# Two-layer graph attention on one core: a small addition after each of layer 0's gathers, and an order made from 16-byte ranges

## The chip, the cores and the metric

The kernel runs on one NeuronCore of a Trainium2 chip. A core has five engines that run their own instruction queues side by side: TensorE (PE, with its weight loads shown as PEld), VectorE (DVE), ScalarE (ACT), GpSimd (POOL) and SyncE (SP, which here only issues transfers). They signal each other through semaphores. Data lies in SBUF (128 partitions), products go to PSUM, and DMA engines move data between SBUF and HBM. The metric is the device time of one execution in microseconds, as the median of several runs.

## The reference, cut to what matters

Two layers on 2708 nodes of width 256, with one dense 2708 x 2708 adjacency matrix in which few entries are not zero:

```python
x = layernorm(x + gnn0(x, adj))    # layer 0
x = layernorm(x + gnn1(x, adj))    # layer 1

def gnn0(h, adj):                  # node_adj and edge_adj are both adj
    d = diag(adj); a = adj with its diagonal set to zero
    edge_output = gru_cell(a @ h, h, edge weights)
    support = mean over 3 heads of  (softmax(mask(e_head), axis=1) * a) @ (h @ W_head)
    node_output = gru_cell(support, h, node weights)
    return d * edge_output + d * node_output
    # a > 0 takes e_plus; entries of a are never negative

def gnn1(x, adj):                  # 4 heads of 64 columns
    h = x @ W;  e = leaky_relu(s_src[i] + s_dst[j]), masked where adj <= 0.5
    return softmax(e, axis=0) summed over i with h, per head
```

The adjacency is sparse and its nonzeros thin out with the node's number, so the kernel finds the rows that a block of columns needs and fetches only those.

## The kernel before, in words

The fast path (a general path stands behind it for other data) has four stages.

*Loading and listing.* The transposed adjacency is read once in three parts of up to 1024 columns (63 large loads on SP's queue). ScalarE and VectorE turn each piece into signs and bits, TensorE makes the softmax logits and denominators. For 51 blocks of columns of layer 0 (`BLOCKS0`) and 32 of layer 1 (`BLOCKS1`), `listed` (line 716) makes lists of the row numbers that are not all zero: counts by a scan and small products, then large comparisons on VectorE (tiles f_lists), products onto `lst` and `rk`, and an index table (`idx`). There are eight such batches for layer 0 and five for layer 1.

*Layer 0's sums.* The blocks are worked off in groups of 512 columns, in the order 4, 3, 2, 1, 0, 5. For each list of 128 rows two gathers are issued on GpSimd, an indirect DMA each: the raw adjacency values of those rows in the block's columns (`fetch_raw`, line 841, into f_raw, or f_ah for the first 16) and the rows of x with their head weights (`fetch_rows`, line 1063, from the table f_T0 into f_xg). There are 131 of each kind. The raw ring holds 40 pieces, the row ring (`xg_ring`, line 625) four buffers of two row sets. `layer0` (line 1074) multiplies on VectorE (tile f_four) and TensorE adds up in PSUM (tiles acc). Blocks with many full rows take the first of them without a gather.

*Cells and norm.* When a group's sums are complete, `cells_and_norm` (line 1130) makes the products with the head weights and the two gated cells (PE tiles side), the gates on ScalarE and VectorE, the layer norm, and layer 1's table f_T1. For each block of 128 nodes GpSimd adds the result to a running sum (f_xacc) and adds a bias (f_low).

*Layer 1.* 96 gathers (`fetch_h`, line 1344) fetch rows of f_T1 into buffers that take the place of the lists, VectorE makes the masked weights (again shown as f_lists), TensorE adds up, and the result is normed and written.

*What sets the order.* The program is not emitted in the order of its text. Every call is kept in an `Order` (its `add` is reached from line 375, which is why the profile shows that line nearly everywhere). `issue` (line 223) finds which call depends on which from the ranges of SBUF that they touch, gives each a duration (`duration`, line 180), and lists all calls by a forward and backward pass repeated twelve times; the best list is emitted, and each engine gets its calls in that order. `spans` (line 134) turns an access into ranges, counted in cells of 32 bytes: two calls that touch the same cell are taken to depend on each other. The synchronisation in the emitted program is made afterwards from the accesses themselves. Calls recorded inside `R.together()` stay next to each other. A gather is taken to cost 1.36 us:

```python
        if engine == "gpsimd":
            if method == "indirect_dma_start":
                return 1.36
            return (n * (4.0 if method == "tensor_add" else 0.8) + 60) / 960.0
```

All gathers go through one helper, `gathered` (line 812), called from the three fetch functions.

Of the kernel before, what the change touches and what calls it, by code (L numbers as in the profile page):

```python
# [14 lines left out]
U32 = mybir.dt.uint32  # L15
# [7 lines left out]
P = 128  # L23
# [49 lines left out]
def _size(ap):  # L73
    n = 1
    for d in ap.shape[1:]:
        n *= d
    return n


def _width(dt):  # L80
    return {F32: 4, I32: 4, U32: 4, BF16: 2, F16: 2, U16: 2, F8: 1}[dt]
# [6 lines left out]
class Order:  # L88
# [44 lines left out]
    @staticmethod  # L133
    def spans(ap):

        name, pat, wide = ap.tensor.name, [tuple(d) for d in ap.ap], _width(ap.dtype)
        if name.startswith("in_"):
            return name, []
        space = str(ap.space)
        if "PSUM" in space:  # L140
            return name, [(0, 1)]
        if "DRAM" in space:
            at, cell = ap.offset, 1024
        else:
            step = pat[0][0]
            at, cell = (ap.offset % step if step else ap.offset), 32
            pat = pat[1:]
        run, outer = 1, []
        for s, n in sorted((abs(s), n) for s, n in pat if s and n > 1):
            if s <= run + cell // wide:  # L150
                run = s * (n - 1) + run
            else:
                outer.append((s, n))
        starts = [at]
        for s, n in outer:
            starts = [a + k * s for a in starts for k in range(n)]
        out = []
        for a in sorted(starts):
            lo, hi = a * wide // cell, (a + run) * wide - 1
            hi = hi // cell + 1  # L160
            if out and lo <= out[-1][1]:
                out[-1] = (out[-1][0], max(hi, out[-1][1]))
            else:
                out.append((lo, hi))
        return name, out
# [14 lines left out]
    def duration(self, call):  # L180
        engine, method, args, kw = call
        outs, ins = self.touched(call)
        out = outs[0]
        n = max([_size(out)] + [_size(a) for a in ins if method in ("tensor_reduce", "bn_stats")])
        if engine == "tensor":
            moving = kw["rhs"] if method == "matmul" else args[1]
            still = kw["lhsT"] if method == "matmul" else args[1]
            cols = _size(moving) if method == "matmul" else P
            if _width(moving.dtype) == 4:
                if method == "transpose":  # L190
                    return 0.2
                return max(4 * cols + 2 * _size(still), 800 if _size(still) > 96 else 500) / 2400.0
            return max(cols, 108) / 2400.0 + 0.01
        if engine == "vector":
            wide = [a for a in outs + ins if _size(a) > 1]
            fast = all(_width(a.dtype) == 2 for a in wide) or (
                method == "tensor_scalar" and all("PSUM" not in str(a.space) for a in wide)
            )
            if method in ("tensor_tensor_scan",):
                n *= 1.5  # L200
            if method == "reciprocal":
                n *= 8
            if method in ("bn_stats", "tensor_reduce", "memset", "copy_predicated"):
                fast = False
            return ((n / 2 if fast else n) + 150 + (60 if method == "scalar_tensor_tensor" else 0)) / 960.0
        if engine == "scalar":
            extra = sum(isinstance(kw.get(k), bass.AP) for k in ("scale", "bias"))
            return (n + 224 + 93 * extra) / 1200.0
        if engine == "gpsimd":
            if method == "indirect_dma_start":  # L210
                return 1.36
            return (n * (4.0 if method == "tensor_add" else 0.8) + 60) / 960.0
        return 0.45

# [185 lines left out]
def fast_path(ctx: ExitStack, tc: tile.TileContext, i: dict, out: bass.AP, bad: bass.AP):  # L400
    nc = tc.nc
    R = Order(nc)
    V, S, G, T, Q = R.vector, R.scalar, R.gpsimd, R.tensor, R.sync
    x, xT_in, adj, adjT = i["x"], i["xT"], i["adj"], i["adjT"]
# [26 lines left out]
    def home(name, shape, dt=F32):  # L431
        return const.tile(shape, dt, name=name)
# [31 lines left out]
    T0 = dram.tile([N, TW0], F32, name="f_T0")  # L464
    T1 = dram.tile([N, TW1], U32, name="f_T1")
# [52 lines left out]
    G.iota(pos_i, pattern=[[P, NB]], base=0, channel_multiplier=1)  # L518
    spans = sorted({(b[2], NB) for b in BLOCKS0} | {(0, NB)})
    pos = home("f_pos", [P, len(spans), NB])  # L520
    past = home("f_past", [P, 1])
    V.tensor_scalar(past, pid, float(size[last]), 1.0e6, op0=ALU.is_ge, op1=MUL)
    for n, (lo, hi) in enumerate(spans):
        V.tensor_scalar(pos[:, n], pos_i, float(-P * lo), None, op0=ADD)
        if lo:
            V.memset(pos[:, n, :lo], 1.0e6)
        V.tensor_add(pos[:, n, last:], pos[:, n, last:], past)
# [53 lines left out]
    column = ({}, {})  # L581
# [9 lines left out]
    idx = [home(f"f_idx{l}", [P, wide_of[l]], I32) for l in (0, 1)]  # L591
# [7 lines left out]
    for l, blocks in enumerate((BLOCKS0, BLOCKS1)):  # L599
        at = l * slots_of[0]  # L600
# [208 lines left out]

    batch_part = [next(k for k, (lo, hi) in enumerate(parts) if lo <= BLOCKS0[b[0][0]][0] < hi) for b in batch0]  # L810

    def gathered(dst, table, ix, at):
        G.indirect_dma_start(dst, None, table, bass.IndirectOffsetOnAxis(ap=ix, axis=0), element_offset=at)

    work0 = []
    for n, (d0, w, q, room_) in sorted(enumerate(BLOCKS0), key=lambda e: (turn.index(e[1][0] // CH), e[0])):
# [16 lines left out]
    def raw_slots(a, b):  # L833
        if b <= early_n:
            return early[:, a:b]
        return raw_all[:, (a - early_n) % raw_n : (a - early_n) % raw_n + b - a]
# [4 lines left out]
    def fetch_raw():  # L841
        k = fetched[0]
        if k == len(work0):
            return False
        n, whole, t = work0[k]
        d0, w = BLOCKS0[n][:2]
        dst = raw_slots(k, k + 1)[:, 0, :w]
        if whole:
            with R.after(loads[1, 16]):
                Q.dma_start(dst, adjT[t * P : (t + 1) * P, d0 : d0 + w])  # L850
        else:
            gathered(dst, adjT, idx[0][:, column[0][n] + t : column[0][n] + t + 1], d0)
        raw_of[k] = dst
        fetched[0] += 1
        return True

    loads, known, seen = {}, [], []
    for g, (c0, c1) in enumerate(parts):
# [12 lines left out]
        for k in range(NB):  # L871
            p = size[k]
            at = at_ring.next()
# [47 lines left out]
    while fetched[0] < raw_n + early_n:  # L921
        fetch_raw()
# [39 lines left out]
    while s0 < len(BLOCKS1):  # L962
        n0 = by_slot[s0]
        d0, w = BLOCKS1[n0][:2]
# [13 lines left out]
    for c, cell in enumerate(("edge", "node")):  # L978
        pair = []
        for wn in ("Wih", "Whh"):  # L980
            t = wts.take([P, KD, 3 * D])
# [73 lines left out]
    while k < len(work0):  # L1055
        n, whole, t = work0[k]
# [6 lines left out]
    def fetch_rows(j):  # L1063
        ks = pairs0[j]
        n, whole, t = work0[ks[0]]
        if whole:
            return
        xg = xg_ring.next()
        for m, k in enumerate(ks):
            t = work0[k][2]  # L1070
            gathered(xg[:, m, :], T0, idx[0][:, column[0][n] + t : column[0][n] + t + 1], 0)
        rows_of[j] = xg

    def layer0(j):
# [188 lines left out]
    for j in range(ahead - 1):  # L1263
        fetch_rows(j)
    for g in turn:
        spread_dens(g)
        for j in steps[g]:
            if j + ahead - 1 < len(pairs0):
                with R.part(f"rows{BLOCKS0[work0[pairs0[j + ahead - 1][0]][0]][0] // CH}"):
                    fetch_rows(j + ahead - 1)  # L1270
            with R.part(f"sums{g}"):
                layer0(j)
            done = pairs0[j][-1] + 1
            check_raw(done)
            with R.part("raw"):
                while fetched[0] < min(max(checked[0], early_n) + raw_n, len(work0)):
                    fetch_raw()
        cells_and_norm(g)
# [65 lines left out]
    def fetch_h(j):  # L1344
        n, ts = work1[j]
        hg = hg_ring.next()
        for m, t in enumerate(ts):
            c = column[1][n] + t
            gathered(hg[:, m, :].bitcast(U32), T1, idx[1][:, c : c + 1], 0)
        hg_of[j] = hg  # L1350

    outs = {}
# [70 lines left out]
    for j in range(ahead1 - 1):  # L1423
        fetch_h(j)
    for j, (n, ts) in enumerate(work1):
        g = BLOCKS1[n][0] // CH
        if g + 1 < NG and g + 1 not in S_of:
            spread_values(g + 1)
        if j + ahead1 - 1 < len(work1):
            fetch_h(j + ahead1 - 1)  # L1430
        layer1(j)
# [455 lines left out]
```

## Time and profile before

| what | value |
|---|---|
| median of three runs | 841.58 us (840.92 to 844.88) |
| the profiled execution | 901.63 us, its span 899.9 us |
| mean granted TensorE clock in it | 0.851 |
| TensorE busy | 678.9 us, 4588 matmul records |
| VectorE busy | 551.1 us |
| GpSimd busy | 436.2 us |
| raw gathers onto f_raw | 115, mean 1.011 us |
| raw gathers onto f_ah | 16, mean 1.005 us |
| row gathers onto f_xg, four buffers | 131, means 1.005 to 1.085 us |
| layer 1's gathers onto f_lists | 96, mean 1.132 us |

The profiled execution is 60 us longer than the median. Times of stages are read from it in microseconds from the start of its span: the loads end near 160, layer 0 runs from there to about 710, layer 1 from about 728 to the end. A line of a timeline has start, length, engine, line, operation, what is written from what, how many, and in brackets the engine's idle time before it with what ended it; "issue" there means that no wait is seen, "remote" that the releaser isn't known. In the list of waits a line has the waiting engine and tile, what it waited for, the sum in us, how often, and the longest.

### The profile page before, as it was taken

The page shows a single profiled execution, that of the slowest core. Times are in us where ns is not written, and L with a number is a line of the kernel's source. Part 1 is how long each engine was busy: PE and PEld are TensorE (multiplying, and loading weights), DVE is VectorE, ACT ScalarE, POOL GpSimd, SP SyncE. Part 2 cuts the span into 40 slices and gives each one's busy share as a digit, 9 for nine tenths or more (in the row PEclk, how much of TensorE's full clock was granted, in tenths as well). Part 3 has the DMA queues.
Part 4 walks back from the last instruction along what each step waited for, and adds up shares of the span by engine and source line. Part 5 has one row for each costly group of instructions (what it writes and reads, how often), then busy time and mean ns, then how long its engine had stood idle before and what let it go on. Part 6 is the DMA issues. An engine that isn't in the chain of part 4 may idle for free. (4 is left out here: it accounts for less than half of the span.)

```text
span 899.9 us, 12878 instructions
## 1 busy us (share of the span) xinstructions
PE 678.9 (75%) x4588; PEld 481.8 (54%) x4588; DVE 551.1 (61%) x1355; ACT 233.0 (26%) x496; POOL 436.2 (48%) x565
## 2 busy tenths in 40 slices
PE   1474764778769899988898879999988565776664
PEld 1463653565335555565555545564467464765553
DVE  7373576695126847763436644561498734977996
ACT  4403664001011321122111121123125301113244
POOL 7006000476725716666677777550005266777830
PEclk9995555588979999999999999999999855787886
DMA  9934886572101312243223222121004244555541
GB/s 300 335 124 144 280 307 186 164 227 59 23 17 47 120 57 51 44 113 84 51 53 91 81 74 74 51 74 42 1 1 130 106 124 124 175 154 169 159 139 47
DMA packets 60647, 103.50 MB, mean 115 GB/s; under 512 B 20887, under 2 KB 37027, under 8 KB 59935
## 3 DMA queue, kind: packets, MB, share of 16 engines
q1 hardware_dynamic: 40337, 61.41, 20.5%
q0 software_dynamic: 17472, 41.15, 17.6%
q8 instruction: 38, 0.62, 0.3%
q10 hardware_dynamic: 2766, 0.04, 0.2%
q14 instruction: 34, 0.28, 0.1%
HBM read 93.07 MB, written 12.27 MB: 117 GB/s over the span
## 5 line engine op out<-in xcount | busy, mean ns | idle before, releaser
L375 POOL DMA_INDIRECT f_raw<-in_adjT_dram,f_idx x115 | 116.2, 1011 | 47.7 <-issue 31.9
L375 PE MATMUL acc<-f_lists 128*65 128x128 f32 (+3 forms) x768 | 100.3, 303 | 51.7 <-DVE f_lists L375 37.9
L375 POOL DMA_INDIRECT f_lists<-f_T,f_idx x96 | 108.6, 1132 | 50.2 <-issue 20.6
L375 PE MATMUL side<-f_xT,f_wts 128*128 128x512 f32 (+1 forms) x288 | 123.0, 553 | 13.0 <-DVE f_big L375 11.9
L375 PE MATMUL side<-f_big,f_wts 128*128 128x512 f32 (+1 forms) x288 | 123.1, 553 | 9.5 <-ACT f_big L375 8.4
L375 PEld LDWEIGHTS acc<-f_lists 128*65 128x65 f32 x768 | 92.0, 189 | 58.4 <-DVE f_lists L375 42.6
L375 PEld LDWEIGHTS side<-f_big,f_wts 128*128 128x128 f32 x288 | 53.1, 194 | 64.4 <-issue 54.9
L375 POOL DMA_INDIRECT f_xg__133<-f_T,f_idx x36 | 39.1, 1085 | 99.5 <-DMA f_T<-f_E 71.6
L375 PEld LDWEIGHTS side<-f_xT,f_wts 128*128 128x128 f32 x288 | 51.0, 191 | 60.7 <-issue 43.3
L375 ACT ACTIVATE f_big<-f_wts 128x1024 fp8e4<-128x1024 f32 (+2 forms) x66 | 61.7, 952 | 48.3 <-DMA f_wts<-in_adjT_dram 39.8
L375 POOL TENSOR_TENSOR f_xacc<-f_xacc,f_low 128x256 f32<-128x256 f32 (+1 forms) x22 | 22.6, 1029 | 96.9 <-ACT f_low L375 96.1
L375 ACT ACTIVATE f_big<-side,f_biases 128x512 f32<-128x512 f32 (+1 forms) x48 | 30.4, 636 | 129.3 <-PE side L375 76.6
L375 DVE TENSOR_TENSOR f_big<-f_big 128x512 f32<-128x512 f32 (+1 forms) x48 | 30.4, 636 | 49.7 <-ACT f_big L375 42.8
L375 DVE TENSOR_SCALAR f_wts<-f_wts 128x1024 fp8e4<-128x1024 f32 (+1 forms) x66 | 43.2, 662 | 25.1 <-DMA f_wts<-in_adjT_dram 23.3
L375 PE MATMUL side<-f_big,f_gat_w 128*128 128x512 f32 (+1 forms) x144 | 56.1, 544 | 2.5 <-DVE f_s_d L375 1.6
L375 DVE TENSOR_TENSOR f_lists<-f_big,f_lists 128x512 f32<-128x512 f32 (+4 forms) x56 | 44.3, 791 | 21.3 <-PE acc L375 6.9
L375 PEld LDWEIGHTS <-f_big 128*128 128x128 fp8e4 x968 | 36.4, 103 | 34.2 <-issue 18.6
L375 POOL DMA_INDIRECT f_xg__135<-f_T,f_idx x33 | 34.7, 1052 | 36.9 <-PE acc L375 24.4
L375 PE MATMUL side<-f_pow,f_wts 128*128 128x8 bf16 x484 | 23.6, 170 | 37.1 <-DVE f_wts L375 35.6
L375 PEld LDWEIGHTS <-f_lists 128*32 128x32 f16 (+6 forms) x617 | 35.4, 134 | 27.1 <-DVE f_lists L375 17.2
L375 PE MATMUL lst<-f_lists 128*128 128x256 f16 (+4 forms) x285 | 37.5, 297 | 16.0 <-DVE f_lists L375 16.0
L375 DVE TENSOR_TENSOR f_lists<-f_iota,f_lists 128x2816 f16<-128x2816 f16 (+5 forms) x26 | 49.4, 1922 | 0.3
(244 smaller groups left out, 1208.2 us busy)
## 6 DMA issues: line engine op xcount, KB each, us to landing
f_wts<-in_adjT_dram SPq DMA_DIRECT2D x42, 512.0 KB
f_wts<-in_adjT_dram SPq DMA_DIRECT2D x21, 330.0 KB
f_big<-f_Rd SPq DMA_DIRECT2D x5, 1024.0 KB
f_big<-f_Sd SPq DMA_DIRECT2D x5, 1024.0 KB
f_T<-f_ah SPq DMA_DIRECT2D x21, 132.0 KB
f_X<-f_low SPq DMA_DIRECT2D x21, 128.0 KB
f_low<-f_X SPq DMA_DIRECT2D x21, 128.0 KB
out_dram<-f_big SPq DMA_DIRECT2D x21, 128.0 KB
```

Source lines behind the costliest of these rows:

```text
L375: getattr(getattr(self.nc, engine_), method)(*args, **kw)
```

## The change

Three edits. `gathered` gets the layer as first argument, and for layer 0 records, together with the gather and right behind it, one addition on GpSimd of a tile f_idle of one partition by 128 elements to itself; the tile is set to zero once at the start. Its accesses are left out of the ranges. In the durations, a gather costs 1.27 us and such an addition 0.45. And `spans` counts SBUF in cells of 16 bytes instead of 32.

```diff
-        if name.startswith("in_"):
+        if name.startswith(("in_", "f_idle")):
             return name, []
...
-            at, cell = (ap.offset % step if step else ap.offset), 32
+            at, cell = (ap.offset % step if step else ap.offset), 16
...
             if method == "indirect_dma_start":
-                return 1.36
+                return 1.27
+            if outs[0].tensor.name.startswith("f_idle"):
+                return 0.45
...
-    def gathered(dst, table, ix, at):
-        G.indirect_dma_start(dst, None, table, bass.IndirectOffsetOnAxis(ap=ix, axis=0), element_offset=at)
+    idle = home("f_idle", [1, P])
+    G.memset(idle, 0.0)
+
+    def gathered(l, dst, table, ix, at):
+        with R.together():
+            G.indirect_dma_start(dst, None, table, bass.IndirectOffsetOnAxis(ap=ix, axis=0), element_offset=at)
+            if l == 0:
+                for _ in range(1):
+                    G.tensor_add(idle, idle, idle)
...
-            gathered(dst, adjT, idx[0][:, column[0][n] + t : column[0][n] + t + 1], d0)
+            gathered(0, dst, adjT, idx[0][:, column[0][n] + t : column[0][n] + t + 1], d0)
...
-            gathered(xg[:, m, :], T0, idx[0][:, column[0][n] + t : column[0][n] + t + 1], 0)
+            gathered(0, xg[:, m, :], T0, idx[0][:, column[0][n] + t : column[0][n] + t + 1], 0)
...
-            gathered(hg[:, m, :].bitcast(U32), T1, idx[1][:, c : c + 1], 0)
+            gathered(1, hg[:, m, :].bitcast(U32), T1, idx[1][:, c : c + 1], 0)
```

## The prediction

> **What bounds the kernel now.** I read the page first (busy shares, then the forty slices), then the waits of each queue, then GpSimd's timeline and the stretches by window.
>
> ```profile
> PE 678.9 (75%) x4588; PEld 481.8 (54%) x4588; DVE 551.1 (61%) x1355; ACT 233.0 (26%) x496; POOL 436.2 (48%) x565
> PE   1474764778769899988898879999988565776664
> POOL 7006000476725716666677777550005266777830
> ```
>
> No engine bounds the whole. Slices 7 to 29 are layer 0, where TensorE is at 8 to 10 tenths and GpSimd at 5 to 7; after slice 30 (layer 1) TensorE falls to 6 and GpSimd rises to 7. So the question is what GpSimd has to spare while TensorE works through layer 0. The window from the first row gather (162.7 us) to the last (599.7 us) says it; its columns are stretch, length, then busy time of PE, PEld, DVE, ACT, POOL:
>
> ```profile
> 162.70:599.70 437.00, 377.33 (x1612) 237.19 (x1609) 244.95 (x609) 80.63 (x182) 273.53 (x269) 0.93 0.29 79
> ```
>
> How the gathers follow each other is in GpSimd's timeline (start, length, what, idle before):
>
> ```profile
> 400.34 0.95 POOL L375 DMA_INDIRECT f_raw<-in_adjT_dram,f_idx  x1 [0.30 <-issue]
> 401.59 0.95 POOL L375 DMA_INDIRECT f_xg__133<-f_T,f_idx  x1 [0.30 <-issue]
> 402.84 0.95 POOL L375 DMA_INDIRECT f_raw<-in_adjT_dram,f_idx  x1 [0.30 <-issue]
> ...
> 531.15 0.97 POOL L375 DMA_INDIRECT f_xg__135<-f_T,f_idx  x1 [0.31 <-issue]
> 532.13 0.74 POOL L375 TENSOR_TENSOR f_xacc<-f_xacc,f_low 128x256 f32<-128x256 f32 x1
> 533.03 0.96 POOL L375 DMA_INDIRECT f_xg__136<-f_T,f_idx  x1 [0.16 <-issue]
> ```
>
> Back to back, a gather comes every 1.25 us: 0.95 of work and a gap of 0.30 that nothing explains. With an addition between two gathers that gap is gone: 0.01 before the addition, 0.16 after it. GpSimd's 437 us are 273.5 of work, about 61 of short gaps (the "issue" waits of 0.30 in its list of waits) and so about 102 of true waiting. Most of that is back-pressure from TensorE, which has not yet freed a row buffer:
>
> ```profile
> POOL f_xg__135 L375 <- PE acc L375: 24.4, 5, 14.1
> POOL f_xg__133 L375 <- PE acc L375: 16.8, 7, 5.1
> POOL f_xg__136 L375 <- PE acc L375: 10.1, 4, 5.0
> POOL f_xg__134 L375 <- PE acc L375: 10.1, 5, 3.3
> ```
>
> So GpSimd runs ahead of TensorE in layer 0, and TensorE, 377 us busy of 437, is what sets its end.
>
> **What the Trainium skill says.** The page "GPSIMD Engine Reference", section "Elementwise — side-by-side cycle accounting", gives a two-input addition about 2.6 cycles an element at 1.2 GHz: 0.28 us for 128 elements, plus a dispatch. The kernel's own additions (128x256: shortest 0.72 to 0.73) agree: 256 elements would be 0.55, and 0.17 remains. Its section "Instruction dispatch" says that all eight cores take every instruction and idle ones still answer, so one partition should not be cheaper than 128; the trace agrees, its two additions over 20 partitions took 0.78 and 0.71 us. Its "Specifications" say that the SBUF interfaces are shared with VectorE, with contention beside some VectorE instructions; the trace shows it: beside VectorE's large list comparisons three additions took 2.20, 3.45 and 2.08 us.
>
> **The change part by part.** (1) 262 additions, one after each of layer 0's 131 raw and 131 row gathers, on one partition by 128 elements, and one memset at the start (about 0.2 us under the first loads; if that cover were gone, 0.2 us). The trace has no such addition. Bounds: 0.10 us (the shortest one-column memsets) and 0.73 us (as much as 256 elements). I take 0.17 + 0.28 = 0.45. Each addition waits for the one before, which a gather lies behind, so the wait is nothing; what queues behind it is the next gather only. Nothing reads its result.
>
> The mean gather of layer 0 from the groups is 1.04 us (246 gathers onto f_raw and f_xg, 254.8 us). Pace before: 1.04 + 0.30 = 1.34. Pace after: 1.04 + 0.01 + 0.45 + 0.16 = 1.66, so 0.32 more. From the first row gather on there are 245 gathers: 245 x 0.32 = 78 us. The 17 before it lie in GpSimd's wait of 71.6 us for the table's write (f_T from f_E), and cost nothing; without that cover they would cost 5.
>
> The 78 us go against 102 of waiting. That would hide all, if all waiting could be given up. It can't: there are four row buffers of two gathers each, so while TensorE does a long block of cell products GpSimd gets at most eight row gathers ahead and stands. I laid the new order's two queues side by side, TensorE's work with the trace's cadences (0.43 us for each of the two passes of a 512-column product, 0.33 to 0.47 for a sum's product), GpSimd's with 1.62 to 1.66 a gather, each row gather held until TensorE is four row pairs behind, its rows usable 5 to 6 us after its start. GpSimd is still held for some 40 us and TensorE comes to stand for 30 us or so; the same sum for the old order gives 6 to 10. TensorE's many other stops (54 us between 175 and 702, of which the sum knows nothing) let GpSimd catch up a little. I take 18 us for the difference: as 78 + 40 - 102 = 16 also says.
>
> (2) The gathers' cost in the order (1.36 becomes 1.27, an addition 0.45) and ranges of 16 bytes only change the order; beside the additions and the memset no instruction is added or removed, the SP queue included, whose rows move past each other but stay the same. On GpSimd the run of 20 raw gathers in a row becomes runs of at most 11, group 4's row gathers stand closer together, and in group 0, the longest, each pair of raw gathers now comes just behind its rows: no lead is left there, so lateness shows at once. On TensorE and VectorE the list batches of layer 1 move up: before the products of group 0's cells there were eight of 22 list products of the first of five batches, now three batches and most of the fourth. The last batch but one no longer stands after the last cell product. What is that worth at the end of layer 0?
>
> ```profile
> 660.00:702.00 42.00, 32.66 (x281) 28.60 (x279) 35.98 (x70) 17.04 (x42) 11.74 (x8) 0.96 0.27 89
> 718.45 0.95 POOL L375 DMA_INDIRECT f_lists<-f_T,f_idx  x1 [2.94 <-PE lst L375]
> 727.03 0.17 DVE L375 TENSOR_SCALAR f_idx<-rk 128x8 int32<-128x8 f32 x1 [5.16 <-remote]
> 728.22 4.05 PE L375 MATMUL acc<-f_lists 128*65 128x32 f32 x35 [6.31 <-DVE f_lists L375]
> ```
>
> VectorE is 36 of 42 us busy there; layer 1's second gather is held from 715.5 to 718.45 for the last lists' products, since both use the same buffer, and its first sums stand behind the last index conversion (727.03). Freed of that, the sums could start about 4 us earlier for the gathers and 5 for the conversion: -9 us, with bounds 0 (the last batch still ends late) and -20 (VectorE's whole load there eased).
>
> The sum: +18 - 9 = +9 us. The profiled execution took 901.63 us (span 899.9), 60 us over the median of 841.58; 901.6 + 9 = 910.6. I add the 9 us as they are: **850 us**, 1% slower. About 0.5% (837.4 to 845.8) is what a measurement can tell from no change.
>
> **Rivals.** *Faster, by late signals relieved.* In the middle of the run of raw gathers other engines get TensorE's signals late:
>
> ```profile
> 238.75 1.88 PE L375 MATMUL side<-f_big,f_wts 128*128 128x512 f32 x4
> 243.81 0.69 DVE L375 TENSOR_TENSOR f_big<-f_big,side 128x512 f32<-128x512 f32 x1 [6.94 <-remote]
> 253.66 1.27 ACT L375 ACTIVATE f_big<-side,f_biases 128x512 f32<-128x512 f32 x2 [8.41 <-remote]
> 254.98 3.78 PE L375 MATMUL side<-f_big,f_wts 128*128 128x512 f32 x4 [8.44 <-ACT f_big L375]
> ```
>
> ScalarE takes at 253.66 a product that TensorE ended at 240.6, and TensorE stands 8.4 us for it. Such "remote" waits come at 412 to 415, 431, 465, 497 and 529 too, each in a dense run of gathers, and none from 600 to 660, where GpSimd issues none. TensorE's stops that follow sum to some 33 us in layer 0. If thinner gathers relieve them, 841.6 + 9 - 33 = 818 to, if half, 834: I say 822. Against it: dense runs at 264 to 275 show no such wait, and the 60 us that profiling adds may be these waits, absent from the median. It decides where more than 9 us of them exist without the profiler and go.
>
> *The additions hide.* At 0.30 us an addition (or a shorter gather without the profiler) the pace is 1.51 and 245 x 0.17 = 42 us lie within what waiting gives up; the moved lists are left: 841.6 - 3 = 838, or no change.
>
> *GpSimd becomes the bound outright.* If VectorE stretches the additions to 0.60, the pace is 1.81, 245 x 0.47 = 115 us, beyond all 102: 115 + 40 - 102 - 9 = 44, so 885.
>
> **How the numbers follow.** Likeliest 0.45 at 850 (its own range 841 to 866); signals relieved 0.22 at 822; hidden 0.20 at 838, evenly faster and same; bound outright 0.13 at 885. Faster: 0.22 + 0.10 = 0.32. Same: 0.10 and a tenth of the likeliest case, 0.15. Slower: 0.53. The range runs from 818 (a third of the relieved case below) to 876 (most of the last case above).
>
> **What would show it.** Additions of 0.4 to 0.5 us and gathers 1.6 us apart; POOL busy near 555 us; fewer "POOL f_xg <- PE acc" waits and new "PE acc <- DVE f_four" or "DVE f_four <- DMA f_xg" waits in group 0 if the pace binds; layer 1's sums following layer 0's last products by 20 us, not 26. Wrong if the "remote" waits of layer 0 vanish and TensorE's busy share there rises; if additions take under 0.3 us; or if VectorE's comparisons stretch them.

## The result, and the profile after

The changed kernel takes 880.95 us (878.51 to 884.24, four runs) beside 843.23 us of before (840.92 to 849.67, four runs): a ratio of 1.047, 95% interval 1.0415 to 1.0525. It is slower by 38 us; 850 had been predicted, in a range of 818 to 876.

One thing is needed to read all that follows: kernels that are compared ran on the same chip beside the kernel before, which takes 841 to 845 us on some chips and 903 to 906 on the others. By its time the trace of before on record (902 us) comes from the latter kind; the comparison and the trace of the changed kernel (878.51 us) come from the former. They are called 842 chips and 904 chips below, and where a number of one kind is set against one of the other, the text says so.

Of the page of the changed kernel, the busy times and the forty slices of TensorE and GpSimd:

```profile
PE 676.8 (77%) x4588; PEld 479.8 (55%) x4588; DVE 569.2 (65%) x1355; ACT 230.3 (26%) x494; POOL 563.0 (64%) x828
PE   1588558799988999899789996649998577756672
POOL 7004905888898359988898889999003277776520
```

GpSimd was mostly at 5 to 7 tenths in layer 0 and is mostly at 8 to 9 now; TensorE has a hole in slices 25 to 27, where group 0's sums are. The window from the first row gather to the last (stretch, length, then busy PE, PEld, DVE, ACT, POOL):

```profile
139.90:607.90 468.00, 404.53 (x1825) 254.20 (x1822) 292.45 (x657) 89.76 (x208) 401.63 (x514) 0.93 0.27 73
```

GpSimd works 402 of 468 us there (274 of 437 before), and another 42 are gaps of at most 0.35 us. Of the waits of layer 0's row gathers little else is left: the table's write ahead of the first of them, and one hold of 22 us for TensorE's sums. The waits for these sums were 61 us in the trace of before.

```profile
POOL f_xg__133 L377 <- DMA f_T<-f_E: 30.5, 1, 30.5
POOL f_xg__133 L377 <- PE acc L377: 22.7, 3, 22.1
...
POOL f_xg__134 L377 <- PE acc L377: 0.5, 3, 0.2
```

The timeline of GpSimd shows the pace (start, length, what, idle before):

```profile
151.41 0.96 POOL L377 DMA_INDIRECT f_xg__136<-f_T,f_idx  x1 [0.16 <-issue]
152.39 0.39 POOL L377 TENSOR_TENSOR f_idle<-f_idle 1x128 f32<-1x128 f32 x1
152.94 0.96 POOL L377 DMA_INDIRECT f_xg__133<-f_T,f_idx  x1 [0.16 <-issue]
...
157.22 2.40 POOL L377 TENSOR_TENSOR f_idle<-f_idle 1x128 f32<-1x128 f32 x1
```

At best a gather comes every 1.52 us instead of 1.25. The addition is 0.39 us at its shortest, but in the groups of instructions (count, then busy time and mean in ns) its mean is 523 ns:

```profile
L377 POOL TENSOR_TENSOR f_idle<-f_idle 1x128 f32<-1x128 f32 x262 | 137.0, 523 | 4.5
```

Who pays is on TensorE's timeline in group 0: products that wait for VectorE's weights (f_four).

```profile
569.89 3.14 PE L377 MATMUL acc<-f_four__137,f_xg__134 128*128 128x208 f32 x8 [4.55 <-DVE f_four__137 L377]
...
590.15 3.78 PE L377 MATMUL acc<-f_four__137,f_xg__133 128*128 128x256 f32 x8 [9.52 <-DVE f_four__137 L377]
```

In the list of waits the weights in turn wait for raw gathers. These are two of its lines; the weights' buffers 138 and 139 have 20.5 and 19.5 us more of the second kind:

```profile
PE acc L377 <- DVE f_four__137 L377: 24.3, 9, 9.5
DVE f_four__137 L377 <- DMA f_raw<-in_adjT_dram,f_idx: 21.5, 14, 4.0
```

It is not the gathers alone. Just ahead of both products shown, a list comparison of 3.1 us stands in VectorE's queue between two instructions for the weights. In the trace of before 16 us of such comparisons come after the last row gather, here 2: the new order has moved them up among the weights.

So after the result the theory was **A**: with the additions GpSimd's pace, the time from one gather to the next, sets the end of layer 0. The rivals: **B**, the new order costs, not the additions; **C**, any instruction between two gathers costs, whatever its length; and later **D**, any interruption costs a fixed price.

### The profile page after: what moved, and what is told of

Read it like the earlier page. It is cut to its first block, busy times and chain, and to the rows that moved or that the text cites. A ratio compares the mean times of both kernels' runs of the same rounds, so it can differ in the third digit from the quotient of the medians.

```text
span 876.6 us, 13148 instructions
## 1 busy us (share of the span) xinstructions
PE 676.8 (77%) x4588; PEld 479.8 (55%) x4588; DVE 569.2 (65%) x1355; ACT 230.3 (26%) x494; POOL 563.0 (64%) x828
## 5 line engine op out<-in xcount | busy, mean ns | idle before, releaser
L377 POOL TENSOR_TENSOR f_idle<-f_idle 1x128 f32<-1x128 f32 x262 | 137.0, 523 | 4.5
L377 POOL DMA_INDIRECT f_lists<-f_T,f_idx x96 | 100.8, 1050 | 51.1 <-issue 19.5
L377 POOL DMA_INDIRECT f_raw<-in_adjT_dram,f_idx x115 | 119.1, 1035 | 18.0 <-issue 16.8
L377 ACT ACTIVATE f_big<-f_wts 128x1024 fp8e4<-128x1024 f32 (+1 forms) x66 | 61.6, 952 | 50.8 <-DMA f_wts<-in_adjT_dram 33.5
L377 POOL DMA_INDIRECT f_xg__133<-f_T,f_idx x36 | 35.9, 997 | 59.5 <-DMA f_T<-f_E 30.5
L377 POOL TENSOR_TENSOR f_xacc<-f_xacc,f_low 128x256 f32<-128x256 f32 (+1 forms) x22 | 18.2, 829 | 72.5 <-ACT f_low L377 71.5
L377 POOL DMA_INDIRECT f_ah<-in_adjT_dram,f_idx x16 | 17.8, 1111 | 63.7 <-DVE f_wts L377 61.4
L377 DVE TENSOR_SCALAR f_wts<-f_wts 128x1024 fp8e4<-128x1024 f32 (+2 forms) x66 | 47.4, 728 | 15.0 <-DMA f_wts<-in_adjT_dram 13.3
L377 ACT ACTIVATE f_big<-acc,f_hm 65x128 f32<-65x128 f32 (+1 forms) x88 | 24.8, 355 | 97.0 <-PE acc L377 81.6
```

Of the source, the lines that this page charges most:

```text
L377: getattr(getattr(self.nc, engine_), method)(*args, **kw)
```

## The experiments

**The additions alone, in the old order; the new order alone; a shorter instruction in the additions' place.** The first takes the kernel before and puts the additions behind the gathers, at no cost in the order, so that every engine keeps its old order:

```diff
             if method == "indirect_dma_start":
                 return 1.36
+            if outs[0].tensor.name.startswith("f_idle"):
+                return 0.0
...
+    def gathered(l, dst, table, ix, at):
+        with R.together():
+            G.indirect_dma_start(dst, None, table, bass.IndirectOffsetOnAxis(ap=ix, axis=0), element_offset=at)
+            if l == 0:
+                for _ in range(1):
+                    G.tensor_add(idle, idle, idle)
```

> The kernel before with the 262 additions and the memset and nothing else: every engine keeps the order of before. Theory A (the additions make GpSimd the engine that sets layer 0's end: a gather every 1.75 us instead of 1.34): most of the 38 us are there, 865 to 890 us, POOL busy near 560 us, and the waits of GpSimd's rows for TensorE's sums gone to under 30 us. Theory B (it is the new order that costs: no lead of raw gathers in group 0, more of layer 1's lists ahead of group 0's cells): 840 to 855.

The second is the changed kernel with no addition, a layer-0 gather costed at 1.72 us (1.27 + 0.45), which leaves every engine the changed kernel's order:

```diff
-                return 1.27
+                return 1.72 if args[2].tensor.name[:4] != 'f_T1' else 1.27
...
             if l == 0:
-                for _ in range(1):
-                    G.tensor_add(idle, idle, idle)
+                pass
```

> The order of the changed kernel on every engine, without the additions. Theory A: 832 to 846, at best the 9 us won that the prediction gave to the moved lists. Theory B: 865 to 885.

The third is the first with one other line:

```diff
-                    G.tensor_add(idle, idle, idle)
+                    G.memset(idle[:, :1], 0.0)
```

> The order of before, and behind each gather of layer 0 a one-column memset in place of the addition: an instruction of some 0.1 us. If it is the length of the additions that costs (theory A), the pace stays near 1.34 us, since the gap of 0.30 gives way to 0.01 + 0.10 + 0.16: 838 to 850. If any instruction between two gathers costs (theory C: without a profiler, gathers follow each other closer than the trace of before shows, and an instruction between them ends that): over 860.

And the kernel before, unchanged, for its trace:

> The kernel before, unchanged, profiled once more. If the late signals of TensorE (the waits called remote, and 60 us between the profiled execution and the median) come from profiling dense runs of gathers, the profile is again over 880 us, with remote waits in layer 0. If they were one execution's accident, the profile lies within 10 us of 842 and has none.

These ran on a 904 chip (before 905.86). The additions alone took 921.12 us, 1.022 (1.013 to 1.031); the order alone 912.63, 1.011 (1.001 to 1.020); the memset 906.84, 1.002 (0.999 to 1.005). Both A's and B's figures, written for 842 us, missed. C falls: 245 memsets of 0.096 us in the stretch cost nothing that could be told, since the gap before the gather shrinks by about as much; the pace stays near 1.25 us in this timeline of the memset kernel:

```profile
412.00 0.94 POOL L377 DMA_INDIRECT f_raw<-in_adjT_dram,f_idx  x1 [0.21 <-issue]
412.94 0.09 POOL L377 MEMSET f_idle<- 1x1 f32 x1
413.24 0.99 POOL L377 DMA_INDIRECT f_xg__133<-f_T,f_idx  x1 [0.22 <-issue]
```

The trace of before, at 900.54 us, again had late signals of TensorE, and the runs of before beside it took 896 to 914: the trace on record was no accident of one execution. Nor did profiling add the 60 us, as the prediction took it: every profiled execution of the experiments lies within 1% of the median of the kernel's runs on that chip.

**The same two once more, and two additions.** The doubled dose has `range(2)` in place of `range(1)`.

> The additions in the order of before, beside a new set of runs of before. Earlier the pair stood at 1.022, with before at 906 us and 45 us of late TensorE signals (remote waits of ScalarE) in its trace. If those waits are the chip's and not the kernel's, a chip without them has before at 842 us and less slack on GpSimd: theory A (GpSimd's pace sets layer 0's end) expects 1.030 to 1.045 there; theory B (the order costs) under 1.020. On a chip with them: again 1.013 to 1.031.

> The changed kernel's order without additions, once more: earlier 1.011 (1.001 to 1.020), its layer 0 longer by some 10 us, and its sums of layer 1 no earlier at their end although they began 8 us sooner behind the last cell. Theory A: 0.99 to 1.01. Theory B: 1.02 or more.

> The order of before with two additions behind each gather of layer 0: another 245 of 0.45 to 0.5 us on GpSimd, 110 to 122 us. If GpSimd alone sets layer 0's end with one addition already (theory A), nearly all of that comes on top: 90 to 120 us over the kernel with one. If the engine still had much slack with one (theory B), under 70.

> The kernel before again, for its trace: layer 0 (first row gather to the last cell product) of 540 us with remote waits if the time is near 900, some 500 to 510 us without them if it is near 842.

Again a 904 chip (903.45): 1.021 (1.015 to 1.026) for the additions, 1.0075 (1.005 to 1.010) for the order. Two additions took 1047.71 us, 1.159 (1.154 to 1.163). The second addition put 124 us on top of 923.9, and the groups give it half of this line, 122 us:

```profile
L377 POOL TENSOR_TENSOR f_idle<-f_idle 1x128 f32<-1x128 f32 x524 | 243.9, 466 | 25.9
```

That is a little more than the 90 to 120 expected. So with one addition in the old order GpSimd has next to nothing left to give: A's bound holds there. The first addition, nearly as long, cost only 15 to 20. The waits of over 0.35 us between GpSimd's instructions, from the first row gather to the last, say why. They sum to 97 to 111 us in the five traces of before on 904 chips (the one on record and four of the experiments), 36 to 37 with one addition and 21 with two. Old and new load fit: the stretch grew from 441 us (mean of five) to 465, with 90 us more load (busy time and short gaps) and 66 less waiting.

The waits also turn round, and by the dose. In that stretch GpSimd's row gathers wait for TensorE's sums for 58 to 68 us in the traces of before, 16 with one addition and 8 with two. VectorE's work on gathered data (f_four and f_lows) waits for it for 23 to 36 us before, 134 to 141 with one addition and 250 with two. This is A's bound seen from both sides.

The runs of the additions alone showed something else. The late signals ("remote" waits of VectorE and ScalarE) of layer 0 were gone: 42 to 64 us of them in the five traces of before, 54.6 with the memset, none or 0.6 with one addition and none with two. In layer 1, which has no additions, they stayed (17 to 56 us). The list of waits of one trace of before (909 us), both layers together, has among others:

```profile
ACT f_big L375 <- remote: 28.8, 6, 10.1
DVE f_idx L375 <- remote: 16.2, 3, 9.7
DVE f_four__139 L375 <- remote: 13.2, 5, 4.0
DVE f_big L375 <- remote: 8.9, 1, 8.9
```

**Half of the additions each, the changed kernel again, and 32-byte ranges.** In the kernel with the additions in the old order, `if l == 0` became `if l == 0 and table is T0` (behind rows alone) or `if l == 0 and table is not T0` (behind raw blocks alone). The last kernel is the changed one with the one line of the ranges undone:

```diff
-            at, cell = (ap.offset % step if step else ap.offset), 16
+            at, cell = (ap.offset % step if step else ap.offset), 32
```

> The changed kernel itself, on a chip of the experiments' kind (before at 903 to 906 us there, with late TensorE signals in layer 0). If additions and order cost what they cost alone (1.021 and 1.008 to 1.011), the product is 1.03: 925 to 937 us. If the late signals make up the 60 us by which before is slower there and the additions remove them (the prediction's first rival), the changed kernel stays near 881, and is faster than before there: 0.97 to 0.98.

> The order of before with additions behind the 131 row gathers alone. Theory A with GpSimd's slack of about 95 us before its pace decides (one addition cost 19 us of its 115, the second 124 of 123): half of the additions, some 58 us, lie within the slack: 0.995 to 1.006. Theory B': additions hold the rows that TensorE waits for, so these cost and those behind raw gathers don't: 1.01 to 1.02.

> The order of before with additions behind the 131 raw gathers alone. Theory A: 0.995 to 1.006 as with the rows. If thinner runs of raw gathers relieve the late signals (remote waits of DVE and ACT in layer 0) and half of the additions fit the slack: 0.97 to 0.99. Theory B': no cost and no gain, 0.997 to 1.003.

> The changed kernel with ranges of 32 bytes: additions and their costs in the order as in the changed kernel. If the 16-byte ranges by themselves bring the costly part of the new order: as the additions alone or better, 1.005 to 1.02. If it is the costs 1.27 and 0.45, or the additions alone: within 0.005 of the changed kernel of the same call.

These ran on an 842 chip (before 840.92 us). The changed kernel: 875.98, 1.042 (1.033 to 1.050). Additions behind the rows alone: 875.64, 1.037 (1.028 to 1.047). Behind the raw blocks alone: 877.77, 1.042 (1.033 to 1.051). The changed kernel with 32-byte ranges: 873.95, 1.037 (1.029 to 1.046). So the ranges make no difference to the time that could be told here, though they change the order. Both halves missed what was expected of them: each cost 35 to 37 us, as much as the whole change. Both kinds of addition cost alike, so B' falls, by which only those behind rows would cost. None of these traces has a single remote wait of VectorE or ScalarE, in either layer, although nothing was added in layer 1: so far as it was seen, these chips have no late signals. The windows from first to last row gather, of the kernel with rows alone:

```profile
151.10:579.60 428.50, 374.76 (x1635) 237.52 (x1632) 251.79 (x614) 81.87 (x186) 338.22 (x399) 0.93 0.29 80
```

and with raw blocks alone:

```profile
153.00:584.70 431.70, 376.09 (x1621) 236.96 (x1621) 249.70 (x611) 80.59 (x182) 325.52 (x383) 0.93 0.29 80
```

In the second of these, waits of over 0.35 us still sum to 52 us, and yet 37 of some 43 us of added load show in the time. So waiting that stands in a list isn't all slack.

**All additions in the old order on an 842 chip.** Either the old order has next to no slack there, so that all additions cost twice what half of them do, or any interruption has a fixed price of 35 us (D). The first of these runs were on a 904 chip, beside one new kernel: no additions, 16-byte ranges, and 1.27 for a gather.

> The additions in the order of before, now hoped for on a chip where before takes 841. Theory A (without late signals the old order leaves GpSimd no slack, each addition costs its 0.3 us, and the new order wins half of that back): 905 to 920 us, 1.075 to 1.095. Theory D (a fixed price for any interruption): 870 to 882. Where before takes 905: 1.02 again.

> The new order without the additions, where before takes 841. Theory A: GpSimd's 246 gathers at 1.34 us bound it no longer as much, 0.96 to 1.00. Theory D: 0.995 to 1.005. If the new order is worse by itself there as where before takes 905: 1.008 to 1.02.

> The trace of before where it takes 841: no remote waits in layer 0, layer 0 (first row gather to the last cell product) of some 500 us instead of 540. Theory A: GpSimd's waits for TensorE's sums in layer 0 (61 us in the trace on record) under 25 us. Theory D: they stay over 40.

> No additions; ranges of 16 bytes, and 1.27 us for a gather in the order in place of 1.36: what the change does to the order without the additions' cost in it. As it moves instructions only: 0.985 to 1.01 under every theory; below 0.99 it would beat both kernels.

Before took 902.51 us there; the additions alone 1.019 (1.011 to 1.027), the order alone 1.013 (1.004 to 1.021), both as before. The kernel without additions in its third order took 937.57 us, 1.036 (1.029 to 1.044), which no theory expected. So an order alone can cost 35 us on such a chip. Its late signals in layer 0 sum to 93 us, but those of the order alone to 91 in the trace beside it, at 1.013; they don't explain the 35 by themselves, and the cause stays open.

Then, on an 842 chip (844.97 us):

> All 262 additions in the order of before, beside before. Where before takes 903: 1.02, as three times already. Where it takes 841: theory A (GpSimd without slack, its pace sets the last row gather, and 103 us of TensorE's work always follow that gather in the old order) expects the same 905 to 920 us as on the other chips, 1.075 to 1.095; theory D (a fixed price) 870 to 882, 1.035 to 1.05.

All additions in the old order took 911.37 us there, 1.078 (1.073 to 1.083), as A had said. D falls, and so does B: the order is the old one, and the price is higher than the whole change's. The halves' 34.7 and 36.9 us sum to 71.6, and together they cost 66.4: the two prices nearly add up. The window from first to last row gather:

```profile
154.70:616.90 462.20, 382.95 (x1605) 240.56 (x1605) 256.35 (x613) 81.64 (x186) 385.56 (x513) 0.90 0.28 74
```

and of the same kernel on a 904 chip, where it takes 923 us:

```profile
156.20:620.50 464.30, 385.56 (x1626) 240.39 (x1624) 259.75 (x614) 81.35 (x186) 386.05 (x514) 0.91 0.27 74
```

With the additions the stretch is the same on both kinds of chip, although before differs by 60 us between them. Of both, 36 to 37 us are waits of GpSimd over 0.35 and the rest is its load; the granted clocks of the two windows, 0.90 and 0.91, are alike too. So GpSimd sets it, and there are no late signals in it on either.

> The kernel before for its trace, hoped for where it takes 841. Half of the additions cost 35 us there and all of them 67, of 45 and 89 us that they put on GpSimd, so it has some 10 to 22 us to give up: its longer waits from the first row gather to the last sum to under 60 us (102 in the trace on record), that stretch takes 390 to 400 us (437 there), and no waits called remote stand in layer 0.

This run was on a 904 chip again (896.75 us, 97 us of waits), so there is no trace of before on an 842 chip. By the other runs: in thirteen traces of the old order 102 to 105 us pass from the end of the last row gather to the end of the last cell product (the last product of f_xT onto side), so the 68 us between the profiled 913 us of the additions and before's 845 lie nearly all in the stretch. That makes before's some 394 us there, 336 of load as in every trace of before and some 58 of waits. The two kernels with half of the additions give 392 and 393 in the same way. This is worked out, not seen.

**What the new order does.** Against the additions in the old order it wins 35 us on 842 chips (911.37 to 875.98), or 31 when each is taken beside its own before. By the traces, 38 us apart, the first row gather starts at 139.6 instead of 154.7 us, 15 earlier; the stretch takes 468 instead of 462; from the last row gather to the last cell product it is 76 instead of 103 us, since more of TensorE's work stands ahead of that gather; and the tail behind the last cell product is 2 shorter. Without additions on 904 chips it loses 6 to 15 us: the same 26 us behind the last row gather are won, but the stretch grows by some 45, as GpSimd is held longer (135 to 148 us of waits over 0.35). These traces have more late signals than before's, too (56 to 91 us in layer 0), so the loss need not be there on an 842 chip. The layer-1 part is seen best here. On GpSimd's and TensorE's timelines of the order alone (920.8 us span):

```profile
736.13 0.96 POOL L377 DMA_INDIRECT f_lists<-f_T,f_idx  x1 [0.96 <-DMA f_Sd<-f_dT__162]
...
741.48 1.97 PE L377 MATMUL acc<-f_lists 128*65 128x32 f32 x16 [4.08 <-DVE f_lists L377]
```

The last cell product ended at 723.4. The first sums follow by 18 us, against 26.6 in the traces of before; but the first gather follows by 12.7, against 12.9 to 13.1. The sums then take 165 to 168 us instead of 158 to 161. What was won at their start is lost, by these lines behind the gathers; no run tested that alone.

## Why the prediction was wrong

*The additions.* 0.45 us, "gathers 1.6 us apart" and POOL busy near 555 us were planned; measured were 0.52 (0.46 in the old order), 1.52 at best and 563.0. Load on the stretch (busy and short gaps, over 245 gathers) went from 1.37 us a gather to 1.81 in the changed kernel, so 108 us and not 78; in the old order to 1.74, 90 us. Some 18 of the 30 us too little are the longer additions. The other 12 are the gaps: they fell by 20 us in all, from 63 to 42, where 0.13 us a gather makes 32. The Trainium skill's price held for the undisturbed addition ("GPSIMD Engine Reference", section "Elementwise — side-by-side cycle accounting": by its rate 0.28 us for the elements, an estimate, to which the prediction added 0.17; measured 0.39). What fits the mean of 0.52 is that page's section "Specifications", by which the SBUF interfaces are shared with VectorE: 49 additions took over 0.60 us, every one of them beside a VectorE instruction, and they hold 33 of the 36 us by which all 262 exceed 0.39 each. The one of 2.40 us in the timeline above is such a one. It was seen, and counted only in a rival.

*The slack, which is the step that failed.* "The 78 us go against 102 of waiting", less some 40 that can't be given up, read the slack from a trace at 902 us and applied it to a kernel that takes 842: "I add the 9 us as they are". On the trace's kind of chip the step came out: 66 us of 103 were given up with 37 left, and the additions alone cost 15 to 21 us where 18 had been said, with some luck, as the load there was 90 and not 78. On an 842 chip the same edit costs 66 us: that is the direct proof that the slack was not there. Where the time was to be predicted, some 58 us of waiting stood (worked out above), and the changed kernel keeps 24: 34 us given up, not 62. So "78 + 40 - 102 = 16" should have been 108 + 24 - 58 = 74. That the waiting missing on 842 chips is what late signals made on the others fits the traces, but is not shown.

*The moved lists.* "-9" ended at its own bound 0. The sums did come 18 us behind the last products ("20 us, not 26"), but the start of layer 1's gathers hardly moved, and the tail from the last cell product to the end is no shorter: 189 and 192.5 us in the two traces of the changed kernel beside 190 to 192 in the old order with additions on 842 chips, and with the order alone 197 to 200 beside before's 196 to 198 on 904 chips.

*What was not priced.* The new order starts the row gathers 15 us earlier and leaves 27 us less behind the last; "no lead is left there, so lateness shows at once" was seen, its other side wasn't. With the sizes put in: 108 - 34 - 15 - 27 = +32, where 38 was measured in that comparison and 35 in the second. As the 58, and with it the 34, comes from before's own time, this sum says where the time lies and is no second proof. It also says that 850 came as near to 881 as it did by luck: 42 us that the prediction left out took back more than half of the 74.

*The rivals.* "GpSimd becomes the bound outright", at 885, was the case that came, but by lack of slack more than by additions of 0.60 us; that its figure is near is luck too, since its sum also has the 102. What "late signals relieved" rests on is real on 904 chips: the additions clear layer 0 of them. Whether that alone gains time isn't shown, since the additions' pace costs more than it could bring. On the 842 chips no trace has any, so it seems that there was nothing to relieve; layer 0 without additions was not traced there. "The additions hide" came true for no run with additions. (Its 838 takes 3 us for the moved lists where the main sum takes 9. And the remote wait that the working puts at 529 stands at 536.)

Open: why a chip is of one kind or the other, and why signals come late; a trace of before on an 842 chip; the new order without additions there. The changed kernel was not run on a 904 chip. As the additions in the old order take 10 to 13 us more there, it might come out near 890, below before's 904; that is only argued. Five chips were met in the experiments, two of the one kind and three of the other, and only one of them, a 904 chip, more than once. No version was found that beats the kernel before.

## What to carry to other kernels

Compare the profiled execution's time with the median first: when they differ by 60 us, waits in the trace may belong to the chip it ran on, and slack read from them is not there. A queue's slack is measured by a dose: small instructions behind half of the gathers cost 36 us and behind all of them 66, and on other chips the first behind each cost some 20 and the second 124; where the price comes near the length of what was added, the slack has ended. And a stage that starts sooner is worth nothing when another queue, here by its timeline the gathers, sets its end.

## What the runs showed of the hardware

The same program takes 841 to 845 us on some chips and 903 to 906 on others, at granted clocks that overlap (0.85 to 0.92 in the runs of before on the former, 0.83 to 0.90 on the latter). Only traces from the latter show other engines getting TensorE's signals late: 17 to 56 us in layer 1 with the additions in the old order, none in six traces from the former. On the latter one addition of 0.39 us or more behind each gather of layer 0 removes its late signals (42 to 64 us before, at most 0.6 after), a memset of 0.09 us doesn't (54.6). An instruction of 0.09 us between two gathers costs nothing that could be told (1.002, 0.999 to 1.005): the gap ahead of the next gather falls from 0.30 to 0.22 us with it.
